# A third buffer for the running totals of key sums in a fused group-norm, attention and residual kernel

## The chip, the core and the metric

The kernel runs on one NeuronCore of a Trainium2 chip. The metric is device time in microseconds. Three runs of the kernel before gave 2168.27, 2169.49 and 2169.48 us, a median of 2169.48 us.

## The reference

The input `x` holds 32 images of 256 channels and 32 by 32 pixels, that is 1024 positions. Each image is group-normalised (32 groups of 8 channels), goes through causal attention with 8 heads of 32 channels, and the normalised input is not what is added back but `x` itself:

```python
q = einsum('oc,bcs->bos', q_w, xf) + q_b          # xf = group norm of x
kv = einsum('oc,bcs->bos', kv_w, xf) + kv_b
k, v = kv[:, :256], kv[:, 256:]                   # then split into 8 heads of 32
mask = tril(ones((S, S)), -1)                     # a query sees earlier positions only
scores = einsum('bhqd,bhkd->bhqk', q, k) / sqrt(32)
scores = where(mask == 0, -10000, scores)
attn = where(mask == 0, 0, softmax(scores))
out = einsum('bhqk,bhkd->bhqd', attn, v)
return x + out
```

All arithmetic is in float32.

## The kernel before, in words

**Work units.** The 8 heads are handled as two groups `g` of four, whose channels fill the 128 partitions. The 1024 queries of an image are two halves `hf` of 512, and the keys are eight blocks `k` of 128. A *step* is one (image, group, half, key block). The first half of a group has 3 steps (`k` = 0, 1, 2), the second has 7 (`k` = 0 to 6), the last key block of each half riding along with `k` = 1 or 5. So there are `N` = 20 steps an image and 640 in all.

**One step.** `scores` (L243) makes the transposed scores of the four heads on PE in two PSUM tiles of two heads each, called `sT`; there are three of these (`ps_s`, L133). ACT then takes the exponential of each tile (L259) into one SBUF tile of 128 partitions by 4 heads by 512 queries. POOL zeroes the masked part of a diagonal block (L265). Two steps later (`LAG`), `values` (L273) multiplies the exponentials with the values on PE into the one PSUM accumulator `acc` (L283), and DVE adds them to the running total of key sums (L288).

**Where the running total lives.** It has no tile of its own. The exponentials of the first key block of a half (`k` = 0) are the start of the total: their tile, tagged `e0`, is added to by L288 for each later block of the half. The tiles of the other blocks are tagged `e` and rotate through four buffers. A tile `e0` is thus alive from its exponentials (L259) to the last reading of the total, in `sums` (L295): there four products with a column of ones on PE (L301, tile `pd`) add the total over the 128 keys, ACT copies the result out (L306, tile `den`), and a DMA on the SP queue sends it to DRAM, from where it comes back spread out, is inverted on DVE (L331) and broadcast to `rb`.

**When the total is read.** `SUMS` = `LAG` + 2 = 4: `sums` of a half is issued four steps after the half's last step, behind that step's `scores` and `values`. A group's first half takes its steps 0 to 2 and has its `sums` at step 6. Its second half takes steps 3 to 9 and has its `sums` at step 13. The next group follows ten steps later with 10 to 12 and 13 to 19. So step 13 begins a second half, allocates an `e0`, and is also the step at whose end the total begun at step 3 is last read.

**The order.** On PE, ACT, DVE and POOL the instructions stand in the order in which the loop at L429 issues them: per step first `scores`, then other work of this step, then `values`, then `sums` where due. Other work is the projections of the next half or image (`pp`, `ppv`, L146; PSUM tile `misc`, of which there is one, shared with `pd`), their evacuation on ACT (L208, L224), the normalisation of a coming image, and the finishing of the image before (L346, L347, L351, and the DMA at L352). The SP queue, which issues nearly all DMAs, isn't in that list: its order comes out of the scheduler.

Of the kernel before, what the change touches and what calls it, by code (L numbers as in the profile page):

```python
# [9 lines left out]
F32 = mybir.dt.float32  # L10
# [7 lines left out]
P = 128  # L18
HD = 32
CPG = 8  # L20
HALF = 512
# [10 lines left out]
def tile_norm_attention_residual(  # L32
# [83 lines left out]
    def unshifted():  # L116
# [13 lines left out]
        epool = tc.alloc_tile_pool(name="epool", bufs=4)  # L130
# [104 lines left out]
        def blocks(hf, k):  # L235

            d = k - hf * BPH
            own = slice(max(d, 0) * P, HALF)
            if d == 1:
                return [(k, own, own), (k + 2, slice(0, P), slice(HALF - P, HALF))]  # L240
            return [(k, own, own)]

        def scores(b, g, hf, k):  # L243
            q, kk = live["q", b, g], live["k", b, g]
            d = k - hf * BPH
            tag = "e0" if k == 0 else "e"
            e = epool.tile([P, 4, HALF], F32, tag=tag, bufs=2 if k == 0 else None, name=f"{tag}_{b}_{g}_{hf}_{k}")
            pairs = [ps_s.tile([P, 2, HALF], F32, tag="sT", name=f"sT_{b}_{g}_{hf}_{k}_{a}") for a in range(2)]
            for kb, cols, of in blocks(hf, k):
                for j in range(4):  # L250
                    rows = slice(HD * j, HD * (j + 1))
                    nc.tensor.matmul(  # L252
                        pairs[j // 2][:, j % 2, cols], lhsT=kk[rows, kb * P : (kb + 1) * P],
                        rhs=q[rows, hf * HALF + of.start : hf * HALF + of.stop],
                        start=True, stop=True, skip_group_check=True,
                    )
            c0 = 2 * P if d == 2 else 0
            for a in range(2):
                nc.scalar.activation(e[:, 2 * a : 2 * a + 2, c0:], pairs[a][:, :, c0:], AF.Exp)  # L259
            if d >= 0:  # L260


                n = 2 if d == 1 else 1
                diagonal = e[:, :, c0 : c0 + n * P].rearrange("p j (n q) -> p j n q", q=P)
                nc.gpsimd.affine_select(  # L265
                    out=diagonal, in_=diagonal, pattern=[[0, 4], [0, n], [1, P]],
                    compare_op=ALU.is_gt, fill=0.0, base=0, channel_multiplier=-1,
                )
                if k == 0:
                    nc.gpsimd.memset(e[0:1, :, 0:1], 1.0)  # L270
            live["e", b, g, hf, k] = e
# [121 lines left out]
        with tc.manual_schedule(engines={ENG.PE, ENG.Activation, ENG.DVE, ENG.Pool}):  # L393
# [35 lines left out]
            for i in range(max(max(at), max(after), len(steps) + LAG) + 1):  # L429
                if i < len(steps):  # L430
                    scores(*steps[i])
                for f in at.get(i, ()):
                    f()
                if LAG <= i < len(steps) + LAG:
                    values(*steps[i - LAG])
                for f in after.get(i, ()):
                    f()
# [159 lines left out]
```

## Time and profile before

| what | value |
|---|---|
| median of three runs | 2169.48 us |
| profiled execution, its own time | 2167.23 us |
| its span, first to last instruction | 2165.3 us |
| PE busy | 2084.0 us (96%) |
| PE weight loads busy | 730.1 us (34%) |
| ACT busy | 1493.4 us (69%) |
| DVE busy | 1478.1 us (68%) |
| POOL busy | 449.4 us (21%) |
| mean granted PE clock | 0.994 |

The profiled execution took 2.25 us less than the median. Each engine's row of the page counts time in which an instruction was under way; PE's matmuls overlap, and a matmul that began and then met a stalled neighbour can be counted through. The page's chain of waits follows the program backwards from its end, and the timeline gives the start of each run of like instructions, with the idle time before it in square brackets and what ended it.

### The profile page before, as it was taken

The page shows a single profiled execution, that of the slowest core. Times are in us where ns is not written, and L with a number is a line of the kernel's source. Part 1 is how long each engine was busy: PE and PEld are TensorE (multiplying, and loading weights), DVE is VectorE, ACT ScalarE, POOL GpSimd, SP SyncE. Part 2 cuts the span into 40 slices and gives each one's busy share as a digit, 9 for nine tenths or more (in the row PEclk, how much of TensorE's full clock was granted, in tenths as well). Part 3 has the DMA queues.
Part 4 walks back from the last instruction along what each step waited for, and adds up shares of the span by engine and source line. Part 5 has one row for each costly group of instructions (what it writes and reads, how often), then busy time and mean ns, then how long its engine had stood idle before and what let it go on. Part 6 is the DMA issues. An engine that isn't in the chain of part 4 may idle for free.

```text
span 2165.3 us, 50543 instructions
## 1 busy us (share of the span) xinstructions
PE 2084.0 (96%) x22030; PEld 730.1 (34%) x22030; DVE 1478.1 (68%) x1480; ACT 1493.4 (69%) x1991; POOL 449.4 (21%) x495
## 2 busy tenths in 40 slices
PE   7999999999999999999999999999999999999994
PEld 2333333333333333333333333333333333333331
DVE  3667766676776677666767766776667676667665
ACT  4777677677766776776777767767767777676773
POOL 1221221212212212212112122122121121221211
PEclk9999999999999999999999999999999999999997
DMA  2011011111111111111110111111111101111101
GB/s 96 3 61 61 35 49 46 56 61 54 39 47 47 61 61 37 47 46 56 61 61 33 47 46 61 62 37 47 46 56 61 61 32 49 44 61 42 37 31 53
DMA packets 56784, 107.78 MB, mean 50 GB/s; under 512 B 14188, under 2 KB 15340, under 8 KB 56556
## 3 DMA queue, kind: packets, MB, share of 16 engines
q1 hardware_dynamic: 54780, 103.56, 13.7%
q8 instruction: 175, 2.87, 0.5%
q10 hardware_dynamic: 1776, 0.92, 0.2%
q14 instruction: 53, 0.43, 0.1%
HBM read 68.82 MB, written 35.64 MB: 48 GB/s over the span
## 4 chain that ended last, share of the span: by engine, by line
PE 80%; ACT 9%; issue 6%; POOL 3%; DMA 1%; DVE 1%; ACTq 0%; POOLq 0%; SPq 0%; DVEq 0%
PE sT L252 23%; PE pp L146 22%; PE acc L283 22%; PE ppv L146 8%; PE pd L301 5%; ACT e L259 5%; POOL e L265 2%; ACT den L306 2%; ACT num L292 1%; ACT k L208 1%; DMA qk_bias<-in_L_conv_q_b_dram 0%; PE pm L146 0%; DVE e L288 0%; DMA rb<-inverses 0%; DVE rb L359 0%
## 5 line engine op out<-in xcount | busy, mean ns | idle before, releaser
L259 ACT ACTIVATE e<-sT 128x1024 f32<-128x1024 f32 (+1 forms) x1280 | 1134.5, 941 | 552.9 <-PE sT L252 348.3
L288 DVE TENSOR_TENSOR e<-e,e 128x2048 f32<-128x2048 f32 (+3 forms) x640 | 1086.0, 1697 | 443.0 <-PE acc L283 324.4
L265 POOL TENSOR_SCALAR_AFFINE_SELECT e<-e 128x512 f32<-128x512 f32 (+1 forms) x384 | 420.1, 1094 | 1672.4 <-ACT e L259 1562.0
L252 PE MATMUL sT<-q,k 32*128 32x512 f32 (+3 forms) x6144 | 754.3, 525 | 6.2 <-ACT k L208 0.8
L283 PE MATMUL acc<-e,v 128*32 128x512 f32 (+3 forms) x6144 | 617.3, 489 | 18.5 <-ACT num L292 10.0
L146 PE MATMUL pp<-xn,wT 128*32 128x512 f32 x4096 | 494.2, 600 | 10.7 <-ACT den L306 8.3
L252 PEld LDWEIGHTS sT<-q,k 32*128 32x128 f32 x6144 | 291.1, 183 | 516.5 <-issue 436.4
L283 PEld LDWEIGHTS acc<-e,v 128*32 128x32 f32 x6144 | 175.1, 110 | 366.0 <-issue 233.1
L146 PE MATMUL ppv<-wT,xn 128*32 128x256 f32 x4096 | 247.6, 382 | 9.1 <-ACT den L306 8.3
L146 PEld LDWEIGHTS pp<-xn,wT 128*32 128x32 f32 x4096 | 107.1, 109 | 293.5 <-issue 174.1
L191 DVE TENSOR_SCALAR xn<-x,mean,rstd 128x512 f32<-128x512 f32 x128 | 73.0, 630 | 175.1 <-POOL rstd L184 175.1
L146 PEld LDWEIGHTS ppv<-wT,xn 128*32 128x32 f32 x4096 | 120.0, 109 | 134.2 <-ACT den L306 57.5
L301 PE MATMUL pd<-e,pick 128*32 128x512 f32 x1024 | 134.2, 596 | 14.1 <-DVE e L288 12.9
L208 ACT ACTIVATE q<-pp,qk_bias 128x512 f32<-128x512 f32 x128 | 88.1, 688 | 38.0 <-PE pp L146 38.0
L347 DVE SCALAR_TENSOR_TENSOR rb<-rb,v_bias_col,x 128x512 f32<-128x512 f32 x129 | 105.7, 819 | 4.6
L208 ACT ACTIVATE k<-pp,qk_bias 128x512 f32<-128x512 f32 x128 | 88.1, 688 | 28.7 <-PE pp L146 26.9
L346 DVE TENSOR_TENSOR rb<-num,rb 128x512 f32<-128x512 f32 x129 | 87.6, 679 | 5.1 <-DMA rb<-inverses 5.0
L306 ACT COPY den<-pd 128x512 f32<-128x512 f32 x128 | 75.5, 590 | 15.5 <-PE pd L301 15.5
L156 DVE BATCH_NORM_STATS2 st<-x 128x6 f32<-128x512 f32 x128 | 81.8, 681 | 5.2 <-DMA x<-in_x_dram 5.2
L224 ACT COPY v<-ppv 128x512 f32<-128x512 f32 x128 | 75.0, 586 | 10.7 <-PE ppv L146 8.5
L292 ACT COPY num<-acc 128x512 f32<-128x512 f32 x128 | 74.9, 585 | 3.7 <-PE acc L283 3.7
L301 PEld LDWEIGHTS pd<-e,pick 128*32 128x32 f32 x1024 | 31.8, 110 | 53.2 <-issue 37.7
(40 smaller groups left out, 155.0 us busy)
## 6 DMA issues: line engine op xcount, KB each, us to landing
x<-in_x_dram SPq DMA_DIRECT2D x64, 512.0 KB
rb<-inverses SPq DMA_DIRECT2D x127, 256.0 KB
out_dram<-rb SPq DMA_DIRECT2D x127, 256.0 KB
sums<-den SPq DMA_DIRECT2D x128, 8.0 KB
rows<-sums SPq DMA_DIRECT2D x31, 32.0 KB
inverses<-inv SPq DMA_DIRECT2D x31, 32.0 KB
wn<-in_L_conv_kv_w_dram ACTq DMA_DIRECT2D x2, 256.0 KB
wn<-in_L_conv_q_w_dram ACTq DMA_DIRECT2D x1, 256.0 KB
```

The costliest lines, as they stand in the source:

```text
L146: nc.tensor.matmul(out[part], lhsT=lhsT[:, part], rhs=rhs, start=start, stop=stop, skip_group_check=True)
L208: nc.scalar.activation(live[key][:, cols], pp, AF.Identity, bias=qk_bias[:, n, g : g + 1], scale=(SCALE, 1.0)[n],)
L252: nc.tensor.matmul(pairs[j // 2][:, j % 2, cols], lhsT=kk[rows, kb * P : (kb + 1) * P], rhs=q[rows, hf * HALF + of.start : hf * HALF + of. ...
L259: nc.scalar.activation(e[:, 2 * a : 2 * a + 2, c0:], pairs[a][:, :, c0:], AF.Exp)
L265: nc.gpsimd.affine_select(out=diagonal, in_=diagonal, pattern=[[0, 4], [0, n], [1, P]], compare_op=ALU.is_gt, fill=0.0, base=0, channel_mu ...
L283: nc.tensor.matmul(acc[HD * j : HD * (j + 1), of], lhsT=live["v", b][:, kb, h * HD : (h + 1) * HD], rhs=e[:, j, cols], start=k == 0, stop= ...
L288: nc.vector.tensor_add(total[:, :, of], total[:, :, of], e[:, :, cols])
L292: nc.scalar.copy(live["num", b][:, g, hf * HALF : (hf + 1) * HALF], acc)
L301: nc.tensor.matmul(pd[HD * j : HD * (j + 1), :], lhsT=pick, rhs=total[:, j, :], start=True, stop=True, skip_group_check=True,)
L306: nc.scalar.copy(den, pd)
L346: nc.vector.tensor_mul(rb[:, g, cols], num[:, g, cols], rb[:, g, cols])
L347: nc.vector.scalar_tensor_tensor(rb[:, g, cols], rb[:, g, cols], v_bias_col[:, g : g + 1], xt[:, g, cols], ALU.add, ALU.add)
```

## The change

The tag `e0` gets three buffers in place of two. Nothing else in the source differs. A buffer is 4 x 512 float32 numbers, 8 KB, in each partition.

```diff
             tag = "e0" if k == 0 else "e"
-            e = epool.tile([P, 4, HALF], F32, tag=tag, bufs=2 if k == 0 else None, name=f"{tag}_{b}_{g}_{hf}_{k}")
+            e = epool.tile([P, 4, HALF], F32, tag=tag, bufs=3 if k == 0 else None, name=f"{tag}_{b}_{g}_{hf}_{k}")
             pairs = [ps_s.tile([P, 2, HALF], F32, tag="sT", name=f"sT_{b}_{g}_{hf}_{k}_{a}") for a in range(2)]
```

On PE, ACT, DVE and POOL each instruction keeps its place; what differs are the semaphores that some wait for. These are ACT's instructions where the second half of image 3's first group begins, before the change (tile numbers are image, group, half, key block; `den_2_3` is the copy of the key sums of image 2's last half, whose total lay in `e0_2_1_1_0`):

```order
L259 ACTIVATE e0_3_0_1_0_2075<-sT_3_0_1_0_0_2076 128x1024 [waits DVE_49,PE_49]
L259 ACTIVATE e0_3_0_1_0_2075<-sT_3_0_1_0_1_2077 128x1024
L306 COPY den_2_3_2099<-pd_2_3_2094 128x512 [waits DMAHW7_49]
L259 ACTIVATE e_3_0_1_1_2102<-sT_3_0_1_1_0_2103 128x1024 [waits PE_49,Pool_49]
L259 ACTIVATE e_3_0_1_1_2102<-sT_3_0_1_1_1_2104 128x1024 [waits PE_49]
L224 COPY v_3_1907<-ppv_3_2_2113 128x512 [waits PE_49]
```

And with the change:

```order
L259 ACTIVATE e0_3_0_1_0_2075<-sT_3_0_1_0_0_2076 128x1024 [waits PE_49]
L259 ACTIVATE e0_3_0_1_0_2075<-sT_3_0_1_0_1_2077 128x1024 [waits PE_49]
L306 COPY den_2_3_2099<-pd_2_3_2094 128x512 [waits DMAHW5_49,PE_49]
L259 ACTIVATE e_3_0_1_1_2102<-sT_3_0_1_1_0_2103 128x1024 [waits DVE_49,PE_49,Pool_49]
L259 ACTIVATE e_3_0_1_1_2102<-sT_3_0_1_1_1_2104 128x1024 [waits PE_49]
L224 COPY v_3_1907<-ppv_3_2_2113 128x512 [waits PE_49]
```

Before, the first exponential waited for DVE and PE once, and the second and the copy `den` needed no PE wait of their own; now each waits for its own PE product.

On the SP queue three DMAs of each image change places, where an image's results go out, a copy of key sums goes to DRAM and a coming image is loaded (`-` before, `+` with the change):

```order
 L310 DMA sums_2_1616<-den_2_0_1614 4x512
-L352 DMA out_0_dram<-rb_1_1599 128x512 x4
-L123 DMA x_5_1955<-in_x_dram 128x1024
+L352 DMA out_0_dram<-rb_1_1599 128x512 x3
 L310 DMA sums_2_1616<-den_2_1_1814 4x512
-L123 DMA x_5_1955<-in_x_dram 128x1024
+L352 DMA out_0_dram<-rb_1_1599 128x512
+L123 DMA x_5_1955<-in_x_dram 128x1024 x2
```

The key sums of an image's second half now go out ahead of the fourth result of the image before, and both halves of the load stand behind them.

## The prediction

> **What bounds the kernel now.** I read the page's chain of waits first, then who waited for whom, then the timeline of the place that both name. The chain's summary:
>
> ```profile
> PE 80%; ACT 9%; issue 6%; POOL 3%; DMA 1%; DVE 1%; ACTq 0%; POOLq 0%; SPq 0%; DVEq 0%
> ```
>
> PE sets the time, and the rest of the end-deciding chain is where PE waits for somebody. The list of waits has one entry that is a count rather than a mixture:
>
> ```profile
> ACT e L259 <- PE pd L301: 200.8, 63, 3.2
> ```
>
> Sixty-three times ACT's exponentials waited for the key-sum product `pd`, over 3 us each. An exponential has no use for `pd`: the only thing that ties them is the buffer. There are 64 second halves (32 images, 2 groups), and all but the first begin while the total of the second half before is still to be read by `pd`, at the end of the same step. With two `e0` buffers that is the buffer they must write. So 63 is every second half but one.
>
> Here is one such place on PE in the timeline (columns: start, duration, engine, line, instruction, count, idle before):
>
> ```profile
> 1024.99 1.14 PE L252 MATMUL sT<-q,k 32*128 32x512 f32 x8
> 1026.06 1.07 PE L283 MATMUL acc<-e,v 128*32 128x384 f32 x16
> 1026.95 1.04 PE L301 MATMUL pd<-e,pick 128*32 128x512 f32 x8
> 1027.92 2.34 PE L252 MATMUL sT<-q,k 32*128 32x512 f32 x8
> 1030.53 1.93 PE L146 MATMUL ppv<-wT,xn 128*32 128x256 f32 x32 [0.27 <-ACT den L306]
> ...
> 1037.68 1.06 PE L283 MATMUL acc<-e,v 128*32 128x512 f32 x8
> 1038.56 1.04 PE L301 MATMUL pd<-e,pick 128*32 128x512 f32 x8
> 1039.53 1.14 PE L252 MATMUL sT<-q,k 32*128 32x512 f32 x8
> 1040.60 1.92 PE L146 MATMUL pp<-xn,wT 128*32 128x512 f32 x16
> ```
>
> The lower four rows are a control that the kernel itself provides: the `sums` of a first half, with the same queue of products around it (values, `pd`, scores, projection) but no `e0` being allocated. From the scores behind `pd` to the projection it takes 1040.60 - 1039.53 = 1.07 us there, and 1030.53 - 1027.92 = 2.61 us at the stalled place. ACT at both:
>
> ```profile
> 1023.82 1.09 ACT L259 ACTIVATE e<-sT 128x512 f32<-128x512 f32 x2
> 1028.06 1.94 ACT L259 ACTIVATE e<-sT 128x1024 f32<-128x1024 f32 x2 [3.15 <-PE pd L301]
> 1029.88 0.59 ACT L306 COPY den<-pd 128x512 f32<-128x512 f32 x1
> 1030.34 1.97 ACT L259 ACTIVATE e<-sT 128x1024 f32<-128x1024 f32 x2
> ...
> 1037.83 1.94 ACT L259 ACTIVATE e<-sT 128x1024 f32<-128x1024 f32 x2 [1.26 <-PE sT L252]
> 1039.67 0.58 ACT L306 COPY den<-pd 128x512 f32<-128x512 f32 x1
> ```
>
> ACT was free at 1023.82 + 1.09 = 1024.91 and stood idle until `pd` ended. Two things then hold PE. The next scores need a third and a fourth `sT` tile of three, so their second pair waits for the first exponential; and the projection needs the one `misc` tile, which the copy `den` empties, and that copy stands behind both exponentials on ACT.
>
> **What the change removes.** With three buffers, a second half's `e0` takes the buffer of a total read seven steps earlier, and the exponentials wait for their scores alone. I place them as the control has them. There the exponentials start 1.22 us after their scores (1037.83 against 1036.61):
>
> ```profile
> 1036.61 1.14 PE L252 MATMUL sT<-q,k 32*128 32x512 f32 x8
> ```
>
> At the stalled place that is 1024.99 + 1.22 = 1026.21, well after ACT is free (1024.91), so both end by 1028.15. `pd` has ended by about 1028.06, when the waiting exponential began, so `den` runs from 1028.15 to 1028.74. The projection can begin behind its scores at 1027.92 + 1.07 = 1028.99, and `misc` has been free for 0.25 us. The second pair of scores finds its `sT` tile free from about 1027.2. So the place should become the control, and PE gains 2.61 - 1.07 = 1.54 us.
>
> The other kind of place, inside an image (the one above lies at an image's start), stalls alike:
>
> ```profile
> 1056.83 1.10 ACT L259 ACTIVATE e<-sT 128x512 f32<-128x512 f32 x2
> 1061.15 1.94 ACT L259 ACTIVATE e<-sT 128x1024 f32<-128x1024 f32 x2 [3.22 <-PE pd L301]
> ...
> 1058.08 1.14 PE L252 MATMUL sT<-q,k 32*128 32x512 f32 x8
> 1061.01 2.34 PE L252 MATMUL sT<-q,k 32*128 32x512 f32 x8
> 1063.62 1.92 PE L146 MATMUL pp<-xn,wT 128*32 128x512 f32 x16 [0.27 <-ACT den L306]
> ```
>
> Again 1063.62 - 1061.01 - 1.07 = 1.54 us, and ACT (free at 1057.93) is 1.37 us early for scores ready at 1058.08 + 1.22.
>
> **The bounds of this term.** From below: the idle time that PE's own rows show is 0.27 us a place, hence 62 x 0.27 = 16.7 us. From above I have nothing larger than the difference of starts, 62 x 1.54 = 95.5 us. I take the upper, because the control is the same run of instructions and its matmuls start 1.07 us apart, while the eight stalled scores are counted busy for 2.34 us in which the weight loads show the gap:
>
> ```profile
> 1062.22 0.30 PEld L252 LDWEIGHTS sT<-q,k 32*128 32x128 f32 x4 [0.91 <-ACT e L259]
> 1063.62 0.16 PEld L146 LDWEIGHTS pp<-xn,wT 128*32 128x32 f32 x8 [1.10 <-ACT den L306]
> ```
>
> Of the 1.10 some 0.76 us is the loads' ordinary spacing (the row of the next projection shows 0.76 without a stall of this kind), so the weight loads put the stall at 0.91 + 1.10 - 0.76 = 1.25 us, a middle value: 62 x 1.25 = 77.5 us. The 63rd place lies in the last image, with no projection behind it; I count 1 us, between 0 and 1.54.
>
> ```profile
> 1066.97 0.13 PEld L146 LDWEIGHTS pp<-xn,wT 128*32 128x32 f32 x4 [0.76 <-ACT num L292]
> ```
>
> [...]
>
> **What is late next.** Behind the projection ACT copies it out and copies `num`, on which the next `acc` waits. At the stalled place exponentials, copy and `num` now end about 1.5 us earlier with PE, and in the stretch before the next such place ACT waits for PE again (1.26 us in the control), so nothing is carried over. DVE's additions, which `pd` needs, are not near:
>
> ```profile
> 1014.75 4.17 DVE L288 TENSOR_TENSOR e<-e,e 128x1536 f32<-128x1536 f32 x3 [1.00 <-POOL e L265]
> 1052.10 1.22 DVE L288 TENSOR_TENSOR e<-e,e 128x1024 f32<-128x1024 f32 x1
> ```
>
> They end at 1018.92 and 1053.32, 8 and 7 us before `pd` starts (1026.95, and about 1060.0). An image loses 3.1 us from its 66, and a margin of 7 us bears that. The moved wait for DVE in the following exponential is for a tile of four buffers whose addition lies in the same finished row. Price: 0.
>
> **The DMAs moved on SP.** The load of a coming image falls behind one issue of key sums and the fourth result:
>
> ```profile
> 999.42 0.43 SPq L123 DMA_DIRECT2D x<-in_x_dram  x1
> 999.95 0.52 SPq L310 DMA_DIRECT2D sums<-den  x1
> ...
> 1029.17 1.28 DVE L156 BATCH_NORM_STATS2 st<-x 128x6 f32<-128x512 f32 x2
> ```
>
> The load is issued some 30 us before DVE reads it, and it loses one issue, about 0.5 us. The key sums go out sooner. The result that goes later has its reader outside the kernel. Price: 0 while that cover of 30 us stands; without it, 0.5 us an image, 16 us.
>
> **The sum.** 95.5 + 1 = 96.5 us from the profiled execution's 2167.23 us gives 2070.7; the median of the runs lies 2.25 us above that execution, so I predict 2073.
>
> **The rivals.**
> *The copy `den` keeps part of the stall.* ACT meets `den` only 0.25 us ahead of PE's need. If the freed exponentials start later than the control's 1.22 us after their scores, every further 0.1 us beyond that margin costs 6 us. At 0.75 us late the place wins 1.54 - 0.5 = 1.04 us: 65 us, 2105. For it speaks the thin margin, against it the control, where the same margin never fails in the rows shown.
> *Only the idle that PE's row shows is won*, because stalled matmuls really were at work for 2.34 us: 16.7 us, 2153. Against it stand the weight loads.
> *No change*: the buffer's old reader still orders the writes, or PE gives the time back at the next boundary on `num`; 2169. The order of waits, in which the exponential no longer names DVE, speaks against the first, the control's slack against the second.
> *Slower: the clock.* A denser PE could be granted fewer pulses. The stretch of 67 to 2119 us, at full clock now, is where it would decide:
>
> ```profile
> 67.00:2119.00 2052.00, 2014.46 (x21338) 705.71 (x21332) 1418.26 (x1402) 1442.98 (x1920) 431.42 (x465) 1.00 0.14 49
> 1036.67:1040.67 4.00, 4.00 (x37) 1.05 (x40) 3.75 (x2) 2.42 (x3) 0.00 (x0) 1.00 0.21 70
> ```
>
> After the gain it is 1955.5 us of PE work; it outgrows 2052 from a clock below 0.953, and at 0.94 it would take 2080, 2073 + 125 = 2198. Against it, the control's four gapless microseconds ran at 1.00. [...]
>
> **How the numbers follow.** My forecast gets 0.86, with 2065 to 2091 as its own range (1.65 us a place, a tenth over the difference of starts for a restart that costs more than I see, to the 1.25 of the weight loads). The `den` rival gets 0.07, PE's idle alone 0.03, no change 0.02, the clock 0.02. The range of 2064 to 2092 is the forecast's with a microsecond of spread and leaves out under 2 in 10. About 0.2% is what a measurement of this kernel can tell from no change; faster by more is 0.86 + 0.07 + 0.03 = 0.96, within it 0.02, slower 0.02.
>
> **What would show it.** ACT's waits on `pd` at L259 gone from the list, where 63 stood; the scores behind each second half's `pd` at 1.14 us and the projection 1.07 us behind them; weight loads without the 0.91; the chain with less ACT at L259 and L306; granted clock 1.00; an image every 63.0 us instead of 66.1. I am wrong if PE's starts there stay over 1.3 us apart, if `den` still releases projections with an idle PE row, or if a new wait of 63 entries takes its place.

## The result: 2071 us, and the profile after

The changed kernel took 2070.99 us in the median of four runs (2069.36 to 2072.12), against 2168.88 us for the kernel before (four runs). The ratio is 0.9549, with a 95% interval of 0.9532 to 0.9565. The forecast was 2073 us.

The profiled execution took 2069.36 us against 2167.23, so 97.9 us less. Its chain of waits, summarised by engine on the page of the changed kernel, has less of ACT in it:

```profile
PE 87%; ACT 4%; issue 4%; POOL 3%; DVE 1%; DMA 1%; ACTq 0%; POOLq 0%; SPq 0%; DVEq 0%
```

PE has 87% of the chain where it had 80%, and ACT and "issue" have 8% where they had 15%. In the list of waits (who waited for whom, total, times, longest) the entry of 63 waits of ACT's exponentials at L259 for `pd` at L301 is gone. So are the two entries in which PE itself waited for `den`, which before read:

```profile
PE pp L146 <- ACT den L306: 8.3, 31, 0.3
PE ppv L146 <- ACT den L306: 8.3, 31, 0.3
```

These are entries of the changed kernel:

```profile
ACT e L259 <- PE sT L252: 454.2, 515, 1.3
...
PEld sT L252 <- ACT e L259: 56.5, 70, 0.8
PEld pp L146 <- ACT den L306: 47.8, 63, 0.8
...
PEld ppv L146 <- ACT den L306: 47.0, 62, 0.8
...
ACT den L306 <- PE pd L301: 14.7, 2, 13.5
```

ACT now waits for scores, 515 times and 454.2 us in all; it is busy for 73% of the span. The weight loads (PEld) of the projections still name `den` 125 times, but at 0.8 us at most: that is the spacing that they have without a stall (0.76 us ahead of the loads for `pp` at 1066.97 us in the kernel before).

The place itself, in the timeline of PE (start, duration, what, count):

```profile
980.02 1.14 PE L252 MATMUL sT<-q,k 32*128 32x512 f32 x8
981.10 1.07 PE L283 MATMUL acc<-e,v 128*32 128x384 f32 x16
981.98 1.04 PE L301 MATMUL pd<-e,pick 128*32 128x512 f32 x8
982.95 1.14 PE L252 MATMUL sT<-q,k 32*128 32x512 f32 x8
984.02 1.93 PE L146 MATMUL ppv<-wT,xn 128*32 128x256 f32 x32
...
1045.98 1.14 PE L252 MATMUL sT<-q,k 32*128 32x512 f32 x8
```

The scores behind `pd` take 1.14 us, not 2.34, and the projection follows 1.07 us behind them, not 2.61. The same place one image later is 1045.98 - 982.95 = 63.03 us on; before, an image took 66.1. ACT at that place:

```profile
978.85 1.09 ACT L259 ACTIVATE e<-sT 128x512 f32<-128x512 f32 x2
981.20 1.94 ACT L259 ACTIVATE e<-sT 128x1024 f32<-128x1024 f32 x2 [1.26 <-PE sT L252]
983.09 0.59 ACT L306 COPY den<-pd 128x512 f32<-128x512 f32 x1
```

The exponentials begin 1.18 us after their scores (981.20 - 980.02) and ACT was 1.26 us early for them, like the control of the prediction.

### The profile page after: what moved, and what is told of

It reads as the page before. It is cut to its first block, busy times and chain, and to the rows that moved or that the text cites. A ratio compares the mean times of both kernels' runs of the same rounds, so it can differ in the third digit from the quotient of the medians.

```text
span 2067.4 us, 50451 instructions
## 1 busy us (share of the span) xinstructions
PE 2009.1 (97%) x22030; PEld 712.0 (34%) x22030; DVE 1474.5 (71%) x1480; ACT 1501.4 (73%) x1991; POOL 449.8 (22%) x495
## 4 chain that ended last, share of the span: by engine, by line
PE 87%; ACT 4%; issue 4%; POOL 3%; DVE 1%; DMA 1%; ACTq 0%; POOLq 0%; SPq 0%; DVEq 0%
PE sT L252 27%; PE pp L146 23%; PE acc L283 23%; PE ppv L146 9%; PE pd L301 5%; POOL e L265 3%; ACT e L259 2%; ACT num L292 1%; ACT k L208 1%; DMA qk_bias<-in_L_conv_q_b_dram 0%; PE pm L146 0%; DVE e L288 0%; DMA rb<-inverses 0%; DVE rb L359 0%; DVE rb L347 0%
## 5 line engine op out<-in xcount | busy, mean ns | idle before, releaser
L259 ACT ACTIVATE e<-sT 128x1024 f32<-128x1024 f32 (+1 forms) x1280 | 1132.5, 937 | 461.1 <-PE sT L252 454.2
L252 PE MATMUL sT<-q,k 32*128 32x512 f32 (+3 forms) x6144 | 684.0, 524 | 0.8 <-ACT k L208 0.8
L252 PEld LDWEIGHTS sT<-q,k 32*128 32x128 f32 x6144 | 273.1, 183 | 458.9 <-issue 384.0
L301 PE MATMUL pd<-e,pick 128*32 128x512 f32 x1024 | 134.2, 596 | 13.3 <-DVE e L288 12.2
L156 DVE BATCH_NORM_STATS2 st<-x 128x6 f32<-128x512 f32 x128 | 81.9, 681 | 5.2 <-DMA x<-in_x_dram 5.2
L301 PEld LDWEIGHTS pd<-e,pick 128*32 128x32 f32 x1024 | 31.8, 110 | 52.4 <-issue 37.7
```

Source lines behind the costliest of these rows:

```text
L156: nc.vector.bn_stats(st[:, c, :], live["x", b][:, g, c * HALF : (c + 1) * HALF])
L252: nc.tensor.matmul(pairs[j // 2][:, j % 2, cols], lhsT=kk[rows, kb * P : (kb + 1) * P], rhs=q[rows, hf * HALF + of.start : hf * HALF + of. ...
L301: nc.tensor.matmul(pd[HD * j : HD * (j + 1), :], lhsT=pick, rhs=total[:, j, :], start=True, stop=True, skip_group_check=True,)
```

## The experiments

Each ratio is to runs of the kernel before that were taken beside the experiment (medians of 2168.27 us, and of 2169.77 us for the two kernels with idle copies).

**The same wait removed without a third buffer.** If the buffer is the whole story, reading the old total sooner should do as much as a new buffer. Here the kernel before keeps two buffers, and the key sums of a second half are issued a step earlier, ahead of the scores that begin the next second half:

```diff
-                        n = first + s + (LAG if last and s == N - 1 else SUMS)
+                        n = first + s + (LAG if last and s == N - 1 else SUMS - hf)
```

> Two buffers as before, but the key-sum products of each second half are issued one step earlier (three steps after its last step in place of four), so that the old total is read before the exponentials that need its buffer. If the whole gain of the change is the wait on a buffer at 63 places, the wait goes without a third buffer too: 2071 us within 5, and no entry of L259 waiting for L301. If the gain came from anything that belongs to the third buffer itself (where tiles lie in memory, the order on the SP queue), this kernel stays near 2169 us.

It took 2081.79 us (2080.24 to 2081.95), ratio 0.9597 (0.9581 to 0.9613). The 63 waits are gone, and nine tenths of the gain is there without a third buffer. So that part doesn't come from where a third buffer lies in memory, nor from the changed kernel's SP order, which this kernel doesn't have either. But it is 10.8 us slower than the changed kernel, twice the 5 us that were allowed. PE's timeline and then ACT's at the place show where that lies:

```profile
986.99 1.07 PE L301 MATMUL pd<-e,pick 128*32 128x512 f32 x8
987.99 1.14 PE L252 MATMUL sT<-q,k 32*128 32x512 f32 x8
989.06 1.07 PE L283 MATMUL acc<-e,v 128*32 128x384 f32 x16
990.06 1.31 PE L252 MATMUL sT<-q,k 32*128 32x512 f32 x8
991.30 1.93 PE L146 MATMUL ppv<-wT,xn 128*32 128x256 f32 x32
...
989.16 1.94 ACT L259 ACTIVATE e<-sT 128x1024 f32<-128x1024 f32 x2 [0.46 <-PE sT L252]
```

With `pd` moved ahead, only the value products lie between the two sets of scores. They now start 990.06 - 987.99 = 2.07 us apart, where the changed kernel has 982.95 - 980.02 = 2.93. The second set needs a `sT` tile that the first exponential gives back, and that began at 989.16 and takes about 1.02 us (the mean of this form is 1026 ns in the kernel before and 1022 ns in the changed one), so it ends about 990.18, just after 990.06. The eight scores at 990.06 take 1.31 us where those at 987.99 take 1.14, and what follows comes 1.24 us behind them in place of 1.07. The next such place in this trace shows nearly the same (1023.02 - 1021.79 = 1.23). If all 63 are like the first, that is 63 x 0.17 = 10.7 us, which is the difference. So `pd`, where it stood, was cover for the exponentials.

**Half of the places.** Only the second halves of each image's first head group have their sums moved up:

```diff
-                        n = first + s + (LAG if last and s == N - 1 else SUMS)
+                        n = first + s + (LAG if last and s == N - 1 else SUMS - (hf if g == 0 else 0))
```

> Two buffers, and the earlier key sums (one step) only for the second half of each image's first head group, so that 32 of the 63 places lose their wait and 31 keep it. If places are independent and worth 1.54 us each: 2168.9 - 31 x 1.54 - 1 = 2120 us within 4. If the places that stay stalled absorb what the others win (the work between them was waiting for something else anyway), clearly above: 2140 to 2169 us. The list of waits should hold 31 entries of L259 on L301.

It took 2125.21 us (2122.71 to 2126.68), ratio 0.9801 (0.9785 to 0.9818), 5.2 us over the figure, where 4 were allowed. The wait stands in the list 31 times, as it should:

```profile
ACT e L259 <- PE pd L301: 97.8, 31, 3.2
```

With the 0.17 us that the way of removing it costs (31 x 0.17 = 5.3) the figure would have been 2125.3. And the 43.1 us won are half of the 86.5 us of the version with all places. So what these places win the others don't lose.

**A part of the lateness.** Two buffers again; the key sums of a second half keep their step but stand between its scores and its value products:

```diff
-                        when(n, lambda b=b, g=g, hf=hf: sums(b, g, hf), after)
+                        when(n, lambda b=b, g=g, hf=hf: sums(b, g, hf), at if hf and not (last and s == N - 1) else after)
```

> Two buffers, and the key-sum products of a second half only one place earlier: in the same step, between its scores and its value products. They then begin about 0.9 us sooner than before, at 1.07 us behind the start of the scores, so the exponentials would start at 27.17 in place of 26.21 (unhindered) or 28.06 (before), and the projection 0.65 us late in place of 1.54. Buffer-wait theory: 62 x 0.89 = 55 us of the gain, 2114 us within 8. If the stall were all or nothing, 2169 or 2071 us. The exponentials still name the key sums as what they wait for, 63 times, at about 2 us each in place of 3.2.

It took 2113.36 us (2113.11 to 2115.46), ratio 0.9744 (0.9728 to 0.976). The list of waits, and the timelines of ACT and of PE:

```profile
ACT e L259 <- PE pd L301: 146.4, 63, 2.4
...
1004.11 1.94 ACT L259 ACTIVATE e<-sT 128x1024 f32<-128x1024 f32 x2 [2.29 <-PE pd L301]
```

```profile
1001.90 1.14 PE L252 MATMUL sT<-q,k 32*128 32x512 f32 x8
...
1004.83 1.48 PE L252 MATMUL sT<-q,k 32*128 32x512 f32 x8
1006.58 1.93 PE L146 MATMUL ppv<-wT,xn 128*32 128x256 f32 x32 [0.27 <-ACT den L306]
```

All 63 waits are still there, shorter, and the projection comes 1.75 us behind the scores: 0.68 us too late, where 0.65 was worked out. The exponentials start 1004.11 - 1001.90 = 2.21 us after their scores, 1.03 us later than the 1.18 of the changed kernel; in the kernel before they start 3.07 us after them (1028.06 - 1024.99), 1.89 later, for a stall of 1.54. Both times the stall is the lateness less 0.35 us. It follows the lateness of the exponentials; it is not all or nothing. Note that PE's idle row reads 0.27 us here as it did at the full stall of 1.54 us.

**How much ACT's idle time covers.** The changed kernel with idle copies on ACT ahead of the exponentials that begin a second half, two of them in one kernel and five in the other (`n`); their result isn't used. The tile `spare` that they write is allocated with the constants, which the excerpt leaves out:

```diff
+            if k == 0 and hf:
+                for _ in range(n):
+                    nc.scalar.copy(spare, wT[:, 0, 0:HALF])
             for a in range(2):
                 nc.scalar.activation(e[:, 2 * a : 2 * a + 2, c0:], pairs[a][:, :, c0:], AF.Exp)
```

> The changed kernel with two idle copies of 128x512 added on ACT (result not used) ahead of the exponentials that begin each second half (64 places). In its trace ACT stands idle there for 1.26 to 1.33 us, waiting for the scores; two copies at the 0.48 to 0.6 us apart at which its copies follow each other take 1.0 to 1.2 us and fit. If the idle time of ACT is the cover, no change: 2071 us within 4. If ACT's 73% load already limits, 62 x 1.0 = 62 us more, 2133 us.

> The same with five copies, 2.4 to 3.0 us, so the exponentials start 1.1 to 1.7 us late. By the prediction's rival on the copy of the key sums, the first 0.25 us are covered and the rest is lost once a place: 62 x 0.85 to 1.45 us, 2124 to 2161 us, with the projection behind the key sums again released by that copy with an idle PE row. If ACT's lateness were made up before PE needs the emptied tile, 2071 us. The ACT work added in all is the same per place as 64 x 2.7 = 170 us, so 2240 us if ACT were the limit.

Two copies: 2070.09 us (2069.61 to 2071.59), no change. Five: 2157.06 us (2155.81 to 2158.2), which gives back most of the gain (ratio to the kernel before 0.9942, 0.9926 to 0.9959). The five took 3.22 us, where 2.4 to 3.0 had been expected. In these kernels the added lines shift the numbers: the exponentials are L263, the scores L253, the projections L147, `den` L310. ACT and PE with five copies:

```profile
1021.43 3.22 ACT L261 COPY spare<-wT 128x512 f32<-128x512 f32 x5
1024.56 1.93 ACT L263 ACTIVATE e<-sT 128x1024 f32<-128x1024 f32 x2
1026.38 0.59 ACT L310 COPY den<-pd 128x512 f32<-128x512 f32 x1
```

```profile
1021.63 1.14 PE L253 MATMUL sT<-q,k 32*128 32x512 f32 x8
...
1024.56 2.19 PE L253 MATMUL sT<-q,k 32*128 32x512 f32 x8
1027.02 1.93 PE L147 MATMUL ppv<-wT,xn 128*32 128x256 f32 x32 [0.26 <-ACT den L310]
```

The exponentials start 1024.56 - 1021.63 = 2.93 us after their scores, 1.75 later than the 1.18 of the changed kernel, and the projection loses 2.46 - 1.07 = 1.39 us. The difference, 0.36 us, is the margin of the copy `den`, as at the other two latenesses; the prediction had 0.25. And 62 x 1.39 = 86.2 us is what the kernel lost (86.1). No wait for an `e0` buffer is involved here: late exponentials alone make the stall, by the way of `sT` and `misc`.

**A version that beats both.** In the changed kernel's chain the next PE stall lies where a half's accumulator is copied out and the next half begins it. PE's timeline and then ACT's, of the changed kernel:

```profile
1009.57 0.71 PE L252 MATMUL sT<-q,k 32*128 32x256 f32 x8
1010.59 1.06 PE L283 MATMUL acc<-e,v 128*32 128x512 f32 x8 [0.30 <-ACT num L292]
...
1009.86 0.58 ACT L292 COPY num<-acc 128x512 f32<-128x512 f32 x1
```

The projections of steps 1 and 11 of each image from the second on are issued behind that step's value products in place of ahead of them, so that PE has them to do while `num` is copied:

```diff
                     for n, f in zip(PROJECT, projections(b)):
-                        when(first + n, f)
+                        when(first + n, f, after if n in (1, 11) else at)
```

> The changed kernel, with the projections of steps 1 and 11 of each image (from the second on) issued behind that step's value products in place of ahead of them, so that PE has a projection of 1.85 us to do while ACT copies out the one accumulator before the next half begins it. In the trace of the changed kernel PE loses 0.27 us (scores at 978.11, values at 979.03, against 0.65 between such starts elsewhere) and 0.37 us (1009.57 to 1010.59) there in each image. If PE's order alone sets the time: 2071 - 31 x 0.64 = 2051 us within 5. If ACT is the limit at these places, the stall moves to the next step's exponentials or projection and the time stays at 2071 us.

It took 2051.51 us (2050.19 to 2053.55), ratio to the kernel before 0.9462 (0.9446 to 0.9478); 2051 was worked out. PE at the same two places, and the chain of waits:

```profile
1000.69 0.71 PE L252 MATMUL sT<-q,k 32*128 32x256 f32 x8
1001.34 1.07 PE L283 MATMUL acc<-e,v 128*32 128x512 f32 x8
...
1031.88 0.71 PE L252 MATMUL sT<-q,k 32*128 32x256 f32 x8
1032.52 1.07 PE L283 MATMUL acc<-e,v 128*32 128x512 f32 x8
```

```profile
PE 97%; DVE 1%; DMA 1%; ACT 1%; issue 0%; ACTq 0%; POOL 0%; SPq 0%; DVEq 0%
```

The products start 0.65 and 0.64 us behind the scores; in the changed kernel, what follows such scores without a wait starts 0.65 us behind them (969.78 - 969.13). And the chain holds almost nothing but PE. POOL's 3% went with the stall too. In the changed kernel the other of the two places names POOL as what ended PE's wait:

```profile
979.03 1.06 PE L283 MATMUL acc<-e,v 128*32 128x512 f32 x8 [0.21 <-POOL e L265]
```

POOL's instruction there ended at nearly the same time as the copy `num` (978.29 + 0.59 = 978.88), but it masks the block after the one that these products read. That they don't need it shows in the faster kernel, where they start before the same instruction of POOL has ended (969.22 + 1.11 = 970.33):

```profile
970.15 1.06 PE L283 MATMUL acc<-e,v 128*32 128x512 f32 x8
...
969.22 1.11 POOL L265 TENSOR_SCALAR_AFFINE_SELECT e<-e 128x1024 f32<-128x1024 f32 x1 [1.30 <-ACT e L259]
```

So `num` it is at both places. In the changed kernel the products start 0.15 us after that copy at the one (979.03 - 978.88) and at the other (1010.59 - 1010.44).

## Why the prediction was right, step by step

**The 63 places.** Right: they vanish from the list. Both kernels have the same 22030 matmuls in the same order, so their starts can be compared one by one: the changed kernel gains 1.53 or 1.54 us at each of the 62 places with a projection behind them.

**1.54 us a place, by the control.** Right: the changed place has the control's starts to a hundredth of a microsecond. The middle bound, 1.25 us from the gaps of the weight loads, and the lower, 0.27 us from PE's idle row, were both too small. The middle one left out the 0.30 us in which the first four loads run: the second pair of heads' scores starts 0.30 + 0.91 = 1.21 us behind the first pair, where without a stall both start together, and 1.21 + 1.10 - 0.76 is 1.55. For the lower one, PE's busy time shows why, in the page's rows of before (the first line) and of the changed kernel:

```profile
L252 PE MATMUL sT<-q,k 32*128 32x512 f32 (+3 forms) x6144 | 754.3, 525 | 6.2 <-ACT k L208 0.8
...
PE 2009.1 (97%) x22030; PEld 712.0 (34%) x22030; DVE 1474.5 (71%) x1480; ACT 1501.4 (73%) x1991; POOL 449.8 (22%) x495
L252 PE MATMUL sT<-q,k 32*128 32x512 f32 (+3 forms) x6144 | 684.0, 524 | 0.8 <-ACT k L208 0.8
```

The same 22030 matmuls are busy 74.9 us less than before, of which the scores account for 70.3 (754.3 to 684.0). Three quarters of what was won had been booked as work. Yet no matmul became shorter: the mean of one is 525 and 524 ns. The stalled eight of before and the same eight of the changed kernel, in the view of the tile `sT` (shortest, median and longest in ns, then first and last start in us):

```profile
L252 PE MATMUL sT<-q,k x8: 587/640/692, 1027.9 to 1029.7; 32*128 32x512 f32 x8
...
L252 PE MATMUL sT<-q,k x8: 587/640/692, 983.0 to 983.5; 32*128 32x512 f32 x8
```

Without a stall the scores of four heads run side by side. At the stall two heads' scores run, and then the other two's, and the row is busy for both turns. So the rival "only PE's idle" was right that matmuls were under way for nearly all of the 2.34 us, and wrong that this time couldn't be won. A single matmul isn't counted as longer because its neighbour is stalled, which had been supposed ahead of the prediction: the median is 640 ns in both views. (The argument rests on the starts.)

**The 63rd place, and the sum.** Taken as 1 us; by the starts it is 1.20, the part of the scores alone, as no projection stands behind it. 97.9 us were won in the profiled executions, 96.5 predicted. The 62 places make 95.2 us and with the 63rd 96.4, so the sum was right term by term. The forecast of 2073 is 2.0 us high by the 1.4 us won beyond the 96.5 and by 0.6 us because the median lies 1.6 us above the profiled execution and not 2.25. Of the 1.5 us that the places don't explain, 0.45 lies in the kernel's first 20 us and most of the rest at its end, where the last DMA of the inverses took 1.41 us in place of 2.18. The chain in order of time (start, duration), of before and then of the changed kernel:

```profile
2132.50 2.18 DMA inverses<-inv
...
2035.90 1.41 DMA inverses<-inv
```

That the change shortened this DMA isn't shown; it is one transfer in one execution of each kernel. One slip of the working: at 1.65 us a place the lower end of the range comes to 2066 us, not 2065.

**What is late next.** Right that nothing is: PE's waits on `num` are 10.0 us in 34 in both lists. One thing is better than said: DVE's waits for the key sums' rows (L325) fell as well, here before and after.

```profile
DVE in_range L325 <- DMA rows<-sums: 34.4, 32, 4.7
...
DVE in_range L325 <- DMA rows<-sums: 7.1, 4, 2.9
```

Of these only the last image's, at the end of the kernel, is on the chain.

**The DMAs moved on SP.** Priced at 0; both halves of a load are issued at 1019.03 us, DVE's statistics (L156) next read an `x` at 1047.23, and the list shows no wait for `x` but the two of the kernel's start, so the cover held:

```profile
1019.03 0.91 SPq L123 DMA_DIRECT2D x<-in_x_dram  x2
```

```profile
DVE st L156 <- DMA x<-in_x_dram: 5.2, 2, 4.8
```

The experiment with two buffers and earlier sums has another SP order again (two results, the key sums, two results, the load) and nine tenths of the gain with it.

**The rivals.** The one on `den` is real as a mechanism but doesn't act here: its margin is 0.35 us and the exponentials are not late. "Only PE's idle" and "no change" fell with the result. For the slower one, the clock: the row of granted clock reads as before, 9 in every slice but the last, and the mean is 0.994 in both kernels; from 67 to 2000 us of the changed kernel it is 1.00. No run shows a clock that falls as PE gets denser, and none shows the 0.94 that this rival was priced at, the author's own supposition: the mean is 0.993 to 0.995 in every run.

## What to carry to other kernels

A tile that doubles as an accumulator lives far longer than its neighbours in the rotation, so count its buffers by the step in which it is last read and not by the last step that adds to it. Look in the list of waits for an engine that waits for an instruction whose result it has no use for: here that was a buffer, and the count of such waits said at how many places. To price a stall on PE, find the same run of instructions elsewhere in the trace without the wait and compare the starts, since the busy and the idle rows can share a stall out between them (here 0.27 us of 1.54 stood in the idle row); where two kernels have the same order, compare their starts one by one.

## What was not expected of the hardware

The idle time that PE's matmul rows show at a stall was 0.26 or 0.27 us at each of three stalls that cost 0.68, 1.39 and 1.54 us by the starts. Most of the rest stands in the row of the scores, which reads 1.48, 2.19 and 2.34 us where it reads 1.14 without a stall: 0.34, 1.05 and 1.20 us more, and the wait for the copy `den` added 0.34 us each time. At the largest of the three the starts of the single matmuls show why: the second pair of heads' scores is 1.21 us behind the first (1029.13 - 1027.92). So in these kernels that row marks the place of a stall and says nothing about its size. And moving `pd` one step up, which removes the wait just as well, costs 0.17 us a place, as the order on PE also decides how much time the exponentials get before their `sT` tiles are wanted back.
